# A four-layer graph network on one core: the layers of a pair of batches put off until beside the next pair's extra block

## The chip, the cores and the metric

The kernel runs on one core of a Trainium2 chip. The time is device microseconds of one execution, the median of three runs: 5891.98 us (5891.88 to 5895.87). One further execution was profiled; it took 5867.21 us, and the profile's span of it, from its first to its last recorded instruction, is 5865.4 us.

## The reference

Sixteen batches of a graph with 1024 nodes and 64 features pass four layers, each with a layer norm before it and a residual sum behind it. The first takes quartiles over neighbours, the other three multiply by the adjacency matrix.

```python
h = jnp.maximum(_layernorm(x), 0.0); x = x + L0(h, adj, nodemask, ...)   # quartiles
h = jnp.maximum(_layernorm(x), 0.0); x = x + L1(h, adj, ...)             # gated messages
h = jnp.maximum(_layernorm(x), 0.0); x = x + L2(t, h, adj, ...)          # tanh messages
h = jnp.maximum(_layernorm(x), 0.0); x = x + L3(h, adj, ...)             # attention

def L0(x, adj, mask, ...):
    nd = thinned(adj, mask)                  # every skip-th neighbour is dropped, both ways
    s = sort(where(nd, x, inf))              # per node and feature
    agg = sum(w * lerp(s, tau * (nv - 1)) for tau, w in zip((.25, .5, .75), (.25, .5, .25)))
    return (relu((x + agg) @ W1 + b1) @ W2 + b2) * mask
def L1(h, A, ...):
    m = relu(relu(h @ W1 + b1) @ W2 + b2); msg = relu(A @ m)
    r, z, n = gates(msg @ W_ih.T, h @ W_hh.T); return (1 - z) * n + z * h
def L2(t, h, A, ...):
    return tanh(concat(h, A @ h) @ W1 + b1) @ W2 + b2
def L3(h, adj, W, a):
    hw = h @ W; lh = leaky_relu(hw); e = (lh @ a_src)[:, None] + (lh @ a_dst)[None, :]
    dj = .8 * adj + .2 * e; att = softmax(where(dj > 0, dj, -1e12), axis=1)
    return relu(att @ hw)
```

## The kernel before

The sixteen batches go as eight pairs. Names of the stages in what follows:

- **sort** (`sort_begin`, `sort_pair`, L732 on): for both batches of a pair at once, a sorting network over the nodes on the vector engine, forward with compares (L771 to L775), then backward through the recorded swaps to get each node's code (L803 to L813). It leaves tables of values and codes in DRAM (`h_d`, `p_d`, `t_d`, `w_d`, `y_d`).
- **prepare** (`neighbours`, L858 on), batch after batch: loads the adjacency matrix (`a`, L872), makes 0/1 neighbours and their running count (L873, L878), transposes the matrix on TensorE and stores it in DRAM (`a_d`, L884 to L890), squares the counts on the scalar engine (L907 to L909), and adds up the thinned, symmetric matrix on TensorE (L928, L934) into `ndT`. L945 is the first step behind the last of a batch's matmuls.
- **select** (`weights`, `select`, L960 on), for both batches of the pair: matmuls of `ndT` with position weights (L1096, into PSUM `comb`), evicted on the scalar engine into `y` (L1104), transposed and turned into signs (L1149, L1151); the vector engine takes maxima over `y` (L1162 to L1178, called *lasts* here), and a second family of matmuls (L1196) with masked copies (L1204) picks the values, which are added into `agg` (L1071, L1073). `compact` (L1226 on) gathers the few nodes that fell outside the window and stores their counts in `x_d`.
- **extras** (L1301 on), once a pair: does those few nodes over the full width, for three statistics, and puts the result into `agg` (L1368).
- **layers** (L1374 on), for each batch: the rest of the first layer and the three others. A batch is one chain: L1471 `o0`, L1485 end of layer 0, a pass over the eight blocks of `a_d` (`adj_block`, L1450; matmuls L1459), gates, L1520 end of layer 1, a second pass, L1536 end of layer 2, L1544, then eight attention blocks, each scalar L1561, vector L1563, scalar L1569, vector L1570, scalar L1575, matmuls L1459, and L1583 `x4` with the store of the output.

Program order for pair `pr`: select(pr), extras(pr), layers of both batches, prepare(pr+1), sort of pr+1, `sort_begin` of pr+2. The engines' queues are not written by hand: a scheduler with this order as priority builds one fixed in-order queue for each engine, so that what is traced later fills places where it finds nothing earlier ready. A tile that takes the place of an older one waits for that one tile's users (`reuse_waits="tile"`).

Pools are laid on a stack, so a stage's pools set what may run beside it. In SBUF, bytes per partition: select's `y` stands at 133952 to 170816; extras' pool `xs` at 138016 to 228864; the two batches' layers have a pool each, `ly0` at 138016 to 181696 and `ly1` at 181696 to 228768. In PSUM, select takes all 8 banks; beside prepare (2 banks) extras takes 6, and the layers take 3 and 2 with one for the sort.

## Time and profile before

| | us |
|---|---|
| median of the runs | 5891.98 |
| profiled execution | 5867.21 |
| its span | 5865.4 |
| vector engine (DVE) busy | 5066.1 |
| TensorE (PE) busy | 4372.7 |
| scalar engine (ACT) busy | 3801.4 |
| GpSimd (POOL) busy | 180.9 |
| DMA moved | 568.23 MB, mean 97 GB/s |

A view by windows gives, for any stretch of the span, the busy time of each engine, the TensorE clock that was granted (1 is full), and the share of the DMA engines. A timeline lists an engine's instructions by start, and in brackets how long the engine had been idle before and which instruction ended that. The wait list sums such idle times by the line that waited and the line that released it. Some lines belong to helpers (`norm` L693 to L703, `transposed` L1408 and L1412, `places` L1019 to L1024, `pick` L1064).

The same cycle comes back eight times. The stretch from one pair's first *lasts* instruction to its last is called a **select stretch** here, the one from there to the next pair's first a **tail**: it holds the end of select, extras, layers, prepare and most of the backward sort.

### The profile page before, as it was taken

To read this page: it belongs to the slowest core of one execution; us is meant where nothing else is said; L and a number is where in the kernel's file an instruction comes from. 1 tells how busy PE (TensorE), PEld (TensorE's weight loads), DVE (VectorE), ACT (ScalarE), POOL (GpSimd) and SP (SyncE) were. 2 spreads that over 40 slices of the span, in tenths; PEclk is the share of its full clock that TensorE was granted. 3 is DMA by queue.
4 is the path that set the end of the run, shared out by engine and by line. 5 is a ranking of instruction groups with operands and counts; after the bars stand their busy time and mean duration, and the time that the engine had idled before them with its cause. 6 is when DMAs were issued, how large, how long until landed. Compare 5 with 4: busy or idle time off the path is not lost.

```text
span 5865.4 us, 114417 instructions
## 1 busy us (share of the span) xinstructions
PE 4372.7 (75%) x45010; PEld 2736.6 (47%) x45010; DVE 5066.1 (86%) x13175; ACT 3801.4 (65%) x5752; POOL 180.9 (3%) x292
## 2 busy tenths in 40 slices
PE   1488677885868857788577876788677895878856
PEld 1355443554435544455434554355443554435532
DVE  9899888988899897998889988899888998877744
ACT  1587657676576855777567666677657775577724
POOL 3000000000000000000000000000000000000000
PEclk5699778997889968899689986899878997789967
DMA  4401273013631056210561125501264013620023
GB/s 127 125 27 41 89 221 116 27 31 124 207 98 36 20 156 217 63 40 29 172 203 45 37 77 168 172 35 34 89 206 132 27 32 120 208 81 19 11 88 127
DMA packets 524420, 568.23 MB, mean 97 GB/s; under 512 B 263808, under 2 KB 413568, under 8 KB 523872
## 3 DMA queue, kind: packets, MB, share of 16 engines
q1 hardware_dynamic: 381472, 476.43, 26.0%
q10 hardware_dynamic: 140064, 81.84, 4.6%
q8 instruction: 355, 5.82, 0.4%
q0 software_dynamic: 2336, 2.57, 0.2%
q14 instruction: 193, 1.58, 0.1%
HBM read 376.95 MB, written 183.76 MB: 96 GB/s over the span
## 4 chain that ended last, share of the span: by engine, by line
PE 27%; DVE 23%; ACT 14%; DMA 10%; issue 3%; SPq 0%; POOL 0%; ACTq 0%; DVEq 0%; POOLq 0%
PE comb L1096 7%; DVE y L1167 5%; PE cand L1196 4%; DMA adjT<-a_d 4%; PE bank L1459 4%; ACT sign L1151 3%; PE comb L1287 3%; DMA a_d<-at 2%; ACT y L1104 2%; DVE cand L1204 2%; DVE att L1570 2%; DVE adjT L1563 1%; DVE y L1162 1%; DVE cum L878 1%; DVE wt L974 1%
## 5 line engine op out<-in xcount | busy, mean ns | idle before, releaser
L1096 PE MATMUL comb<-wt,ndT 128*128 128x512 fp8e5 x6144 | 1422.3, 383 | 119.5 <-ACT sign L1151 98.1
L1104 ACT ACTIVATE y<-comb,qb 128x512 int16<-128x512 f32 x1152 | 742.5, 711 | 479.4 <-PE comb L1096 479.0
L1096 PEld LDWEIGHTS <-ndT 128*128 128x128 fp8e5 x6144 | 587.6, 98 | 837.4 <-issue 196.9
L1196 PE MATMUL cand<-vtab,sign 128*128 128x48 f16 (+1 forms) x18432 | 678.8, 192 | 60.9 <-DVE agg L1071 32.4
L1196 PEld LDWEIGHTS <-sign 128*128 128x128 fp8e5 x18432 | 651.5, 97 | 118.6 <-issue 57.2
L1151 ACT ACTIVATE sign<-comb,lower 128x1024 fp8e5<-128x1024 int16 (+1 forms) x640 | 693.2, 1083 | 0.0
L1151 ACT ACTIVATE sign<-comb,half 128x1024 fp8e5<-128x1024 int16 (+1 forms) x640 | 688.0, 1075 | 0.0
L1167 DVE TENSOR_TENSOR y<-y 128x512 uint16<-128x512 uint16 (+5 forms) x896 | 668.7, 788 | 16.6 <-PE comb L1149 16.2
L1204 DVE COPY_PREDICATED cand<-w_f,cand 128x256 f32<-128x256 uint16 (+1 forms) x1536 | 533.7, 376 | 95.8 <-PE cand L1196 92.6
L886 ACT COPY at<-pk 128x512 f32<-128x512 f32 x256 | 147.4, 586 | 394.5 <-PE pk L884 219.0
L1149 PE MATMUL comb<-ident_b,y 128*128 128x128 bf16 x4608 | 318.1, 222 | 93.5 <-ACT sign L1151 59.6
L1459 PE MATMUL bank<-adjT,nd 128*64 128x512 f32 x1024 | 314.1, 668 | 77.6 <-DMA adjT<-a_d 75.7
L1149 PEld LDWEIGHTS <-y 128*128 128x128 bf16 x4608 | 294.6, 99 | 118.9 <-issue 117.9
L928 PE MATMUL pk<-minus_b,rem 128*128 128x128 bf16 x1024 | 225.3, 246 | 158.2 <-ACT rem L909 158.2
L1459 PE MATMUL bank<-att,hs 128*64 128x512 f32 x512 | 199.9, 863 | 155.0 <-ACT hs L1575 154.9
L928 PE MATMUL pk<-ident_b,ni 128*128 128x128 bf16 x1024 | 220.5, 243 | 122.0 <-ACT ndT L934 65.0
L878 DVE TENSOR_TENSOR_SCAN cum<-ni 128x1024 f16<-128x1024 fp8e5 x128 | 291.8, 2283 | 11.0 <-POOL ni L874 10.9
L884 PE MATMUL pk<-ident,a 128*128 128x128 f32 x1024 | 189.5, 336 | 136.8 <-DMA a<-in_adj_dram 102.5
L974 DVE TENSOR_SCALAR wt<-node 128x2048 uint8<-128x2048 f16 x224 | 268.8, 1216 | 13.9 <-PE comb L1287 13.7
L774 DVE TENSOR_TENSOR s<-s 128x512 f32<-128x512 f32 (+1 forms) x440 | 275.6, 626 | 0.0
L1162 DVE TENSOR_SCALAR y<-y 128x4608 int16<-128x4608 int16 x128 | 173.4, 1355 | 118.0 <-ACT y L1104 117.7
L775 DVE TENSOR_TENSOR s<-s 128x512 f32<-128x512 f32 (+1 forms) x440 | 274.4, 624 | 0.0
(373 smaller groups left out, 8301.5 us busy)
## 6 DMA issues: line engine op xcount, KB each, us to landing
adjT<-a_d SPq DMA_DIRECT2D x384, 512.0 KB
a<-in_adj_dram SPq DMA_DIRECT2D x128, 512.0 KB
a_d<-at ACTq DMA_DIRECT2D x256, 256.0 KB
m_d<-swapped SPq DMA_DIRECT2D x104, 512.0 KB
swapped<-m_d SPq DMA_DIRECT2D x104, 512.0 KB
n_d<-nat SPq DMA_DIRECT2D x128, 128.0 KB
x_d<-xr SPq DMA_DIRECT2D x48, 256.0 KB
comb_x<-x_d ACTq DMA_DIRECT2D x24, 512.0 KB
```

The source lines that it names most:

```text
L774: nc.vector.tensor_tensor(to_lo, lo, hi, op=ALU.max)
L878: nc.vector.tensor_tensor_scan(cum[:, t - t0, :], ni[:, t, :], wide[:, t, pad - 1 : pad - 1 + N], 0.0, op0=ALU.add, op1=ALU.add)
L928: nc.tensor.matmul(pk[:, n % 4, :], lhs, rhs, start=(n % 4 == 0 and m == 0), stop=(m == len(terms) - 1 and last),)
L974: nc.vector.tensor_scalar(wt[g][:, :, k : k + 4, :].bitcast(U8), node, 4.0 * (25 + CODE * (8 * g + k)), 4.0 * 26, op0=ALU.add, op1=ALU.min,)
L1096: nc.tensor.matmul(pw, ndT[:, j, t * P : (t + 1) * P], wt[1 + g8][:, j].rearrange("p w c -> p (w c)"), start=(j == 0), stop=(j == NT - 1),)
L1104: nc.scalar.activation(y[:, 0, chunks, at : at + 8 * d_].rearrange("p q (w d) -> p q w d", d=d_), pw.rearrange("p (w q d) -> p q w d", w=8 ...
L1149: nc.tensor.transpose(pt[:, q - q0, :], y[:, 0, q, :].bitcast(BF16), ident_b)
L1151: nc.scalar.activation(signs[tl][s][:, q0:q1, :], pt.bitcast(I16), AF.Sign, bias=before[s], scale=-1.0, saturate=False,)
L1167: nc.vector.tensor_tensor(v[:, :, :, :n], v[:, :, :, :n], v[:, :, :, n : 2 * n], op=ALU.max)
L1196: nc.tensor.matmul(cand[:, e, at : at + 12 * d_].rearrange("p (d l) -> p d l", l=12), signs[tl][sec][:, chunk, :], tab[:, q, :, half_ * 12 ...
L1204: nc.vector.copy_predicated(v[:, :, :, dst : dst + k], mk.to_broadcast([P, 2, C // 2, k]), v[:, :, :, frm : frm + k])
L1459: nc.tensor.matmul(po[to : to + C, :], lhs, rhs[:, f * HALF : (f + 1) * HALF], start=(j == 0), stop=(j == NT - 1))
```

## The change

Extras, layers and the loop over the pairs are rewritten.

- The layers of pair `pr-1` are traced in the tail of pair `pr`, ahead of extras(pr), then prepare and sort as before. In tail 0 there are no layers. In the last tail extras(7) comes first, then the layers of pair 6 with a pool for each batch; behind it the layers of pair 7, again with two pools.
- Where layers run beside extras there is one layer pool, `ly0` (SBUF 132832 to 175808, 2 PSUM banks), which both batches use in turn; extras has `xs` at 175808 to 228320 and 3 banks.
- `agg` goes to DRAM at the end of extras (`g_d`) and is loaded again in layers; `a_d` holds 6 batches, not 4. `rz` takes `att`'s tile; `ones_b` shrinks to 128 columns.
- Extras reads `x_d` in pieces of at most 1024 columns, once for each statistic (12 loads for 4), evicts it in 4 pieces for 1, turns signs in 2 halves for 1, has one `y_x` for two, and works its six sums in groups of four and two: `places` runs twice on narrower words, which lie in the buffers of `comb_x`, and each sum's matmuls and masked copies go in two halves.

What the engines' queues look like afterwards, by the order of the built program: in a middle tail the vector engine has the end of select, then `o0` of the first batch, that batch's chain to `x4` interleaved with extras' first group, prepare and backward sort, then `o0` of the second batch and its chain to `x4` with extras' second group, the rest of prepare, the next pair's weights (L974) and the forward sort of the pair after next, then the first *lasts*. On TensorE the next pair's first L1096 stands behind the transposes (L1581) of the second batch's `x4`; before, L1096 and the second batch's attention matmuls alternated. In a middle pair the scheduler puts 56 us of sort into the select stretch where it put 80 us, and 24 us more into the tail (by the mean durations of before).

```diff
@@ gnn_stack @@
-    a_d = dram.tile([4, NT, P, N], F32, name="a_d")
+    a_d = dram.tile([6, NT, P, N], F32, name="a_d")
+    g_d = [dram.tile([P, NT, C], F32, name=f"g_d{k}") for k in range(4)]
@@ extras @@
-        comb = xs.tile([P, NW * C], F32, name="comb_x")
-        for u in range(0, len(PIECES), 2):
-            nc.scalar.dma_start(comb[:, at], x_d[:, at])
+        def wide():
+            return xs.tile([P, N], F32, name="comb_x", bufs=2)
...
+        def evicted(k):
+            y = xs.tile([P, 2, 2 * NQ, 4 * NH], I16, name="y_x")
+            for u in range(0, len(PIECES), 2):
+                n = len(PIECES[u : u + 2]) * 512
+                comb = wide()[:, :n]
+                nc.scalar.dma_start(comb, x_d[:, PIECES[u] * 512 : PIECES[u] * 512 + n])
+                nc.scalar.activation(y[...], comb.rearrange(...), AF.Identity, bias=qx[:, k : k + 1], scale=1.0)
+            return y
+        def turned(y):
+            signs = [xs.tile([4 * NH, NQ, P], F16, name="sign_x", bufs=4) for s in range(2)]
+            for q0 in range(0, NQ, 8):
+                pt = xp.tile([P, 512], F32, name="tr")...
+                for q in range(8):
+                    nc.tensor.transpose(pt[: 4 * NH, q, :], y[:, 0, q0 + q, :].bitcast(BF16), ident_b)
+                for s in range(2):
+                    nc.scalar.activation(signs[s][:, q0 : q0 + 8, :], pt[: 4 * NH].bitcast(I16), AF.Sign, ...)
+            return signs
...
-        marks = places(xs, z, 6 * C, 1)
-        for s in range(6):
-            cand = xp.tile([P, NQ, P], F32, name="cand")
+        for ks in (range(2), range(2, 3)):
+            for k in ks:
+                y = evicted(k)
+                signs += turned(y)
+                last_of(k - ks[0], y, z, odd)
+            spare = [wide().bitcast(U16) for part in range(-(-10 * nf // (2 * N)))]
+            marks = places(Words(spare, ...), z, nf, 1)
+            for s in range(2 * len(ks)):
+                for q0 in range(0, NQ, 8):
+                    cand = xp.tile([P, 8, P], F32, name="cand")
...
+            if pr + 1 < B // 2:
+                nc.sync.dma_start(g_d[(pr * 2 + i) % 4], aggs[i])
@@ layers @@
+        if agg is None:
+            agg = big()
+            nc.sync.dma_start(agg, g_d[b % 4])
-        rz = ly.tile([P, NT, 2 * C], F32, name="rz")
+        rz = ly.tile([P, N], F32, name="att", bufs=2).rearrange("p (t k) -> p t k", k=2 * C)
@@ the loop over the pairs, behind select @@
-            with nb_ as nb, nbp_ as nbp:
-                with ...(name="xs") as xs, ...(name="xp") as xp:
-                    taken = extras(pr, kept, aggs, xs, xp)
-                with ...("ly0"), ...("ly1"), ...("lb0", bufs=3), ...("lb1", bufs=2), ...("sop", bufs=1):
-                    for i, (ly, lb) in enumerate(((ly0, lb0), (ly1, lb1))):
-                        layers(pr * 2 + i, (pr * 2 + i) % 4, aggs[i], ly, lb)
-                    if pr + 1 < pairs:
-                        made = prepare(pr + 1, nb, nbp)
-                        sort_pair(pr + 1, cur, sop)
-                    if pr + 2 < pairs:
-                        cur = sort_begin(pr + 2, sop)
+        with ExitStack() as beside:
+            final = pr + 1 == pairs
+            if not final:
+                nb, nbp, sop = ...
+            pools = [layer_pools(beside, k, 2) for k in range(2 if final else 1)] if waiting else []
+            xs, xp = ...
+            if final:
+                taken = extras(pr, kept, aggs, xs, xp)
+            if waiting:
+                layers_of(*waiting.pop(), *pools)
+            if not final:
+                taken = extras(pr, kept, aggs, xs, xp)
+                made = prepare(pr + 1, nb, nbp)
+                sort_pair(pr + 1, cur, sop)
+                if pr + 2 < pairs:
+                    cur = sort_begin(pr + 2, sop)
+            waiting.append((pr, aggs if final else [None, None]))
+    with ExitStack() as beside:
+        layers_of(*waiting.pop(), *[layer_pools(beside, k, 4) for k in range(2)])
```

## The prediction

> **What bounds the kernel now.** I read the page's busy line first, then the windows by stage, then the waits inside a tail, then two timelines.
>
> ```profile
> PE 4372.7 (75%) x45010; PEld 2736.6 (47%) x45010; DVE 5066.1 (86%) x13175; ACT 3801.4 (65%) x5752; POOL 180.9 (3%) x292
> ```
>
> No engine is full; the vector engine (DVE) is nearest. The windows below are start:end, length, then busy time of PE, PEld, DVE, ACT, POOL, the granted TensorE clock, DMA share, GB/s. Row 298 is select stretch 0, 641 tail 0, 982 select stretch 1; 2055 and 2392 are a tail and a select stretch of the middle; 5208 is the last select stretch, 5559 the end.
>
> ```profile
> 298.00:641.00 343.00, 298.98 (x3732) 195.34 (x3731) 325.86 (x838) 267.15 (x432) 1.84 (x2) 0.98 0.10 30
> 641.00:982.00 341.00, 234.94 (x1881) 138.89 (x1881) 292.79 (x787) 202.03 (x279) 15.12 (x26) 0.77 0.57 177
> 982.00:1352.00 370.00, 313.16 (x3747) 203.63 (x3745) 335.52 (x858) 272.62 (x442) 1.82 (x3) 0.93 0.09 29
> 2055.00:2392.00 337.00, 229.61 (x1882) 137.00 (x1882) 289.23 (x774) 198.72 (x273) 15.73 (x26) 0.77 0.57 176
> 2392.00:2760.00 368.00, 310.72 (x3744) 201.49 (x3744) 338.76 (x867) 275.69 (x446) 2.02 (x3) 0.94 0.10 32
> 5208.00:5559.00 351.00, 308.49 (x3752) 199.68 (x3751) 264.42 (x715) 276.22 (x447) 1.14 (x2) 0.94 0.06 16
> 5559.00:5865.00 306.00, 184.57 (x1159) 91.75 (x1159) 146.01 (x430) 106.72 (x126) 4.08 (x7) 0.67 0.33 104
> ```
>
> To be seen: DVE idles 48 us in a middle tail (86% busy) and 29 in a select stretch. Select stretch 0, which has no layers beside it, takes 343 with DVE 95% busy; the last takes 351 though DVE has 61 us less to do. So a select stretch is set by its own chain of PE, ACT and DVE, not by the sort work that fills it; what makes the middle ones 368 to 371 is the end of the layers that reaches into them. This is the next view, PE's timeline (start, length; idle before in brackets): the second batch's attention matmuls alternate with the next pair's first matmuls, which evens out two chains that wait for other engines.
>
> ```profile
> 2373.03 0.59 PE L1096 MATMUL comb<-wt,ndT 128*128 128x512 fp8e5 x2
> 2375.04 1.08 PE L1459 MATMUL bank<-att,hs 128*64 128x512 f32 x4 [1.42 <-ACT hs L1575]
> 2376.06 6.65 PE L1096 MATMUL comb<-wt,ndT 128*128 128x512 fp8e5 x30
> 2390.24 0.61 PE L1124 MATMUL comb<-ident_b,ndT 128*128 128x128 bf16 x8
> 2411.11 1.11 PE L1581 MATMUL bank<-ident,srcT 128*128 128x128 f32 x4 [0.70 <-ACT srcT L1578]
> ```
>
> DVE's waits in 2205 to 2392 (waiter, releaser, total us, times, longest) are steps of the layers' chains, though filler stands all around them:
>
> ```profile
> DVE xs L1485 <- PE bank L1478: 5.7, 2, 2.9
> DVE rn L1516 <- ACT rz L1514: 4.9, 4, 1.7
> DVE xs L1536 <- PE bank L1436: 4.2, 1, 4.2
> DVE att L1570 <- ACT att L1569: 2.7, 4, 1.6
> ```
>
> The chain itself, in DVE's timeline of the end, where only the other batch is beside it: `o0`, ends of layers 1 and 2, L1544, `x4`.
>
> ```profile
> 5668.61 0.68 DVE L1471 TENSOR_TENSOR nd<-nd,agg 128x512 f32<-128x512 f32 x1
> 5726.20 0.69 DVE L1520 TENSOR_TENSOR xs<-nd 128x512 f32<-128x512 f32 x1 [0.70 <-ACT nd L1518]
> 5763.47 0.69 DVE L1536 TENSOR_TENSOR xs<-bank,xs 128x512 f32<-128x512 f32 x1 [7.80 <-PE bank L1436]
> 5773.23 0.69 DVE L1544 SCALAR_TENSOR_TENSOR hT<-mT 128x512 f32<-128x512 f32 x1 [4.75 <-ACT mT L1542]
> 5822.22 0.69 DVE L1583 TENSOR_TENSOR nd<-bank,xs 128x512 f32<-128x512 f32 x1 [0.52 <-PE bank L1581]
> ```
>
> That is 154 us; in tails 0 to 6 the first batch took 172, 162, 166, 158, 166, 165, 163 and the second, about 10 us behind, 188 to 196. One batch's chain is thus nearly half a tail, and before, two ran side by side.
>
> **The change, part by part**
>
> *Middle tails (1 to 5).* Both batches now use one pool, so the second `o0` comes after the first `x4`: two chains in series. The start moves forward: `o0` stands in DVE's new order right behind the end of select; the last L1073 of select starts 38 us into the tail (2093.5), so I take 40 (before: 2206.7, 152 in). First chain: the rows give 163 with the other batch beside it; now extras and prepare are beside it. Between its `o0` and `x4` the new order has 155 us of DVE work (every instruction by its mean duration of before), at the 95% of select stretch 0 again 163. Second chain: the shortest of each step over the sixteen batches (9.1, 1.2, 33.7, 7.2, 37.3, 9.7, 49.0) add up to 147; DVE's work there, 120 us, does not bind. Between them 5 us (the order has 7 us of work from `x4` to `o0`). Then the next pair's first L1096, behind L1581 in PE's new order; and the new `y` lies over `ly0`, so its eviction would wait for `x4` in any order. From the first L1096 to L1124, about the first *lasts*, are 17 us above. Sum 40 + 163 + 5 + 147 + 17 = 372. Bounds: 345 (DVE's 331 us of work in this tail at 96%; 24 of its 41 us more are sort that left the select stretch, some 15 layers and weights that did, the rest extras) and 395 (chains of 172 and 160). Five tails: 1860 against 334 + 337 + 332 + 339 + 339 = 1681, +179. Tail 6 has no next sort to begin, the chains are the same: 370 against 332, +38.
>
> *Select stretches 1 to 7.* No layers reach in, and less sort: like stretch 0, 342 each (bounds 335 and 352, the last's). 2394 against 370 + 369 + 368 + 367 + 368 + 371 + 351 = 2564, −170.
>
> *Tail 0.* Layers leave; prepare sets it. Pair 1's first batch reaches L945 at 776, 135 into the tail; the second was 79 behind the first at the start (181 and 260), where no layers ran: 214. Then qb's few steps, first matmuls, 17: some 36. 250 against 341, −91; DVE's work, 226, fits. Bounds 235 and 265.
>
> *The end.* Layers(6) run beside extras(7) in two pools: start 25 in, second batch 190 (its 185 of the last pair, and some for extras): 215. DVE's order puts pair 7's first L1485 behind pair 6's last `x4`, so layers(7) follow whole: from L1485 (5677.9) to the end, 187. 402 against 306, +96. Bounds 380 and 420.
>
> *Extras.* Per pair DVE gets 62 instructions more, at half widths. From L1064 (955 ns at 768 columns, 419 at 256) a column costs 1.05 ns, so the added fixed parts are 60 to 90 ns each: +4 us, inside the 331. ACT: L1325 (3.28 us at 3584) and L1335 (1.96 at 2048) give 0.19 us fixed, so 9 + 6 pieces add 3; 8 more issues at L1307's 0.55 add 4; ACT is busy 199 of 337, so nothing on the path. But the loads now stand in ACT's queue, each waiting for one of two buffers, and the layers' ACT steps are queued behind them; L1325 waited 10.9 us for a landing in six pairs. What hides such waits is ACT's free time, 138 us of a tail; without that cover they cost what the third rival does. SP gets four transfers of 256 KB a pair (`g_d`), written a whole select ahead of their use: nothing; their bound is one landing, 5 us a tail.
>
> *ACT table loads* go from 88 to 100 in the program. By the row of L697 (1283 ns, and 20.4 us idle before 40) that is 12 × 1.8 = 22 us in all, spread over chains: inside the bounds. The Trainium skill, "ScalarE: Activation LUTs", section What ACT_TABLE_LOAD costs, counts a drain too, 2.66 us in all; by it the 12 cost 32 us (an estimate). The idle before the rows is less than that drain.
>
> *A rule that speaks against my sum.* The tail's DVE is busy 86%, the highest of any engine there. The Trainium skill, "Trace Analysis", section Optimization Strategy, says that a kernel with several regimes may gain by interleaving them, and it works from the engine with the highest occupancy; by it the tails would shrink towards DVE's work, 5 × 331 and 302 in tail 6, and the span to 5644 (an estimate). I go by the rows: layers were interleaved already, and DVE still waited on their steps.
>
> **Sum.** +179 + 38 − 170 − 91 + 96 = +52: a span of 5917. The median of the runs is 26.6 above the profiled span (5891.98 − 5865.4), which I add: 5944.
>
> **The rivals**
>
> 1. *DVE packs the tail.* With three independent chains around it filler never lacks, and a tail is DVE's work at the 95.5% of stretch 0: 331 / 0.955 = 347, tail 6 325. Then +54 − 7 − 170 − 91 + 96 = −118: median 5774. For it: extras' stretch 2130 to 2202 is 94% busy. Against: two chains of 147 leave no such tail unless they overlap, and one pool and the order forbid it. It decides where a middle tail is below 361.
> 2. *It cancels:* tails of 362, the same as rival 1 half true: within 12 us of 5892.
> 3. *ACT's queue stalls.* The 12 loads hold ACT until a buffer is free and the third statistic's until DVE's marks in those buffers are used; the first chain stops with it. Loads of this kind took 5 to 8 us in the chain of waits (2098.6: 5.8; 1392.5: 8.0); half of 12 × 6 exposed is 36 a tail, six tails: +216, median 6160; a third of it 6015. For it: ACT's queue is in order. Against: 138 us of free ACT time in a tail.
> 4. *The change does not do what it says* is excluded by the built order.
>
> **How the numbers follow.** About 0.2%, 12 us, is what a measurement of this kernel can tell from no change. Forecast (slower, some 30 to 90 us): 0.53. Rival 1: 0.23. Rival 2: 0.08. Rival 3: 0.16. So faster 0.23, same 0.08, slower 0.69. Six tails at ±14 and seven select stretches at ±5 are ±90 around 5944; with part of the rivals: 5845 to 6050.
>
> **What would show it.** Right: middle tails of 360 to 385 with DVE idle some 40 in them; second `o0` just behind the first `x4`; first L1096 behind the second `x4`; select stretches 335 to 350; an end near 400. Wrong: a lone chain of 130 or less (tail near 345), or idle ACT before L1325's loads in tens of us. If select stretches stay at 368 though no layers reach in, the sort or PE's clock set them, and the sum rises by 180.

## The result and the profile after

The changed kernel takes 6137.93 us (median of four runs, 6118.97 to 6147.62) beside 5891.93 us of the kernel before: a ratio of 1.0419, 95% interval 1.0397 to 1.0442. It is 4.2% slower; the forecast was slower by 0.9%. The profiled execution has a span of 6140.1 us.

Line numbers of the changed kernel are 3 higher in the sort, select and neighbours (L1096 is now L1099, L1162 is L1165); in the layers L1471 is now L1517 (`o0`), L1485 is L1531, L1581 is L1627, L1583 is L1629 (`x4`), and the extras' load and eviction are L1330 and L1331.

The page's busy line after, to be held against the one of before:

```profile
PE 4481.0 (73%) x45010; PEld 2738.8 (45%) x45010; DVE 5114.3 (83%) x13671; ACT 3860.9 (63%) x5884; POOL 201.7 (3%) x292
```

DVE's work grew by 48 us in 275 us of span: the time is in waits. The windows after (start:end, length, busy time of PE, PEld, DVE, ACT, POOL, granted clock, DMA share, GB/s) are, in this order, tail 0, select stretch 1, a middle tail, the select stretch behind it and the end:

```profile
645.00:896.00 251.00, 138.31 (x1486) 103.78 (x1487) 226.49 (x593) 134.59 (x196) 11.01 (x20) 0.65 0.51 151
896.00:1244.00 348.00, 304.01 (x3741) 198.16 (x3737) 326.49 (x841) 267.58 (x433) 2.01 (x3) 0.96 0.10 30
2724.00:3127.00 403.00, 255.25 (x1926) 146.16 (x1926) 332.25 (x905) 217.12 (x309) 18.71 (x26) 0.71 0.54 166
3127.00:3470.00 343.00, 301.59 (x3704) 196.05 (x3701) 302.32 (x798) 265.42 (x428) 2.38 (x3) 0.96 0.08 25
5681.00:6140.00 459.00, 306.55 (x1565) 132.41 (x1565) 230.56 (x756) 190.33 (x247) 6.46 (x13) 0.72 0.43 137
```

Taken from the first and last *lasts* themselves, tail 0 lost 90 us (342 to 251.5) and select stretches 1 to 7 lost 178 together (2555 to 2378). Against that stand six tails of 399 to 403 (before 333 to 340), +386, and the end of 459 (before 306), +153. The sum is +271; select stretch 0 adds 3, and the spans differ by 275. (The forecast's rows of before begin a select stretch about 1 us early, so it has 2564 for 2555 and, for the six tails, 2013 for 2021.) In the middle tail DVE is busy 332 of 403 us, 82%, where it was 86% before.

DVE's timeline of this tail (start, length) shows `o0` and `x4` of the first batch, the same of the second, and the first *lasts* of the next select:

```profile
2773.77 0.69 DVE L1517 TENSOR_TENSOR nd<-nd 128x512 f32<-128x512 f32 x1 [6.52 <-DMA nd<-g_d]
...
2944.79 0.69 DVE L1629 TENSOR_TENSOR nd<-bank,xs 128x512 f32<-128x512 f32 x1 [1.52 <-PE bank L1627]
...
2952.51 0.69 DVE L1517 TENSOR_TENSOR nd<-nd 128x512 f32<-128x512 f32 x1 [0.35 <-DMA nd<-g_d]
...
3114.60 0.69 DVE L1629 TENSOR_TENSOR nd<-bank,xs 128x512 f32<-128x512 f32 x1
...
3127.38 1.35 DVE L1165 TENSOR_SCALAR y<-y 128x4608 int16<-128x4608 int16 x1
```

The tail is one row of steps: 50 us, a chain of 171, 8 us, a chain of 162, 13 us. The second `o0` comes 8 us behind the first `x4`. PE's timeline at the end of the second chain has the next pair's first comb matmul starting half a microsecond behind the start of its last transposes:

```profile
3113.20 0.66 PE L1627 MATMUL bank<-ident,srcT 128*128 128x128 f32 x4 [0.70 <-ACT srcT L1624]
3113.70 4.48 PE L1099 MATMUL comb<-wt,ndT 128*128 128x512 fp8e5 x20
```

### The profile page after: what moved, and what is told of

It is laid out like the page before. It is cut to its first block, busy times and chain, and to the rows that moved or that the text cites. A ratio compares the mean times of both kernels' runs of the same rounds, so it can differ in the third digit from the quotient of the medians.

```text
span 6140.1 us, 115258 instructions
## 1 busy us (share of the span) xinstructions
PE 4481.0 (73%) x45010; PEld 2738.8 (45%) x45010; DVE 5114.3 (83%) x13671; ACT 3860.9 (63%) x5884; POOL 201.7 (3%) x292
## 3 DMA queue, kind: packets, MB, share of 16 engines
q0 software_dynamic: 2336, 2.57, 0.2%
## 4 chain that ended last, share of the span: by engine, by line
PE 36%; DVE 30%; ACT 17%; DMA 13%; issue 3%; POOL 0%; SPq 0%; ACTq 0%; DVEq 0%; POOLq 0%
PE comb L1099 12%; DMA adjT<-a_d 6%; PE cand L1199 6%; ACT sign L1154 5%; DVE y L1170 5%; PE bank L1502 4%; PE comb L1290 4%; DVE cum L881 3%; ACT y L1107 2%; DMA a_d<-at 2%; DVE att L1616 2%; DVE cand L1207 2%; DVE adjT L1609 1%; DVE s L777 1%; DVE s L778 1%
## 5 line engine op out<-in xcount | busy, mean ns | idle before, releaser
L1099 PE MATMUL comb<-wt,ndT 128*128 128x512 fp8e5 x6144 | 1427.5, 385 | 111.7 <-ACT sign L1154 95.7
L1099 PEld LDWEIGHTS <-ndT 128*128 128x128 fp8e5 x6144 | 591.7, 98 | 824.1 <-issue 195.9
L1199 PE MATMUL cand<-vtab,sign 128*128 128x48 f16 (+1 forms) x18432 | 666.4, 191 | 43.2 <-DVE agg L1076 29.2
L1199 PEld LDWEIGHTS <-sign 128*128 128x128 fp8e5 x18432 | 637.4, 96 | 102.0 <-issue 37.1
L1502 PE MATMUL bank<-att,hs 128*64 128x512 f32 x512 | 232.0, 1009 | 355.9 <-ACT hs L1621 355.8
L1502 PE MATMUL bank<-adjT,nd 128*64 128x512 f32 x1024 | 363.8, 796 | 127.2 <-DMA adjT<-a_d 122.8
L1165 DVE TENSOR_SCALAR y<-y 128x4608 int16<-128x4608 int16 x128 | 173.4, 1355 | 184.9 <-ACT y L1107 184.4
L977 DVE TENSOR_SCALAR wt<-node 128x2048 uint8<-128x2048 f16 x224 | 264.7, 1218 | 14.9 <-PE comb L1290 14.6
L778 DVE TENSOR_TENSOR s<-s 128x512 f32<-128x512 f32 (+1 forms) x440 | 274.3, 623 | 0.0
```

The source lines that it names most:

```text
L778: nc.vector.tensor_tensor(to_hi, lo, hi, op=ALU.min)
L1099: nc.tensor.matmul(pw, ndT[:, j, t * P : (t + 1) * P], wt[1 + g8][:, j].rearrange("p w c -> p (w c)"), start=(j == 0), stop=(j == NT - 1),)
L1199: nc.tensor.matmul(cand[:, e, at : at + 12 * d_].rearrange("p (d l) -> p d l", l=12), signs[tl][sec][:, chunk, :], tab[:, q, :, half_ * 12 ...
L1502: nc.tensor.matmul(po[to : to + C, :], lhs, rhs[:, f * HALF : (f + 1) * HALF], start=(j == 0), stop=(j == NT - 1))
```

## The experiments

Each kernel ran beside the kernel before on the same chip. Ratios are to that kernel; where none is given there was one run. "Tail", "select stretch" and "end" are as in the forecast, and "period" is a middle tail with the select stretch behind it: 705 us in the kernel before, 741 in the changed one. Means of five are over tails 1 to 5 and the select stretches behind them.

### What sets a tail

**no_second** leaves out the layers of the odd batch of pairs 0 to 5.

```diff
-        for i in range(2):
+        for i in range(2 if len(pools) > 1 else 1):
             layers(pr * 2 + i, (pr * 2 + i) % 6, aggs[i], *pools[i % len(pools)])
```

> The changed kernel without the layers of the second batch of pairs 0 to 5 (their rows of the output are not computed): the six late tails hold one chain in place of two. Theory (two chains in series set the tail): each of the six tails loses a whole second chain until another limit is met, 401 down to about 305, total about 5570 us. Rival (the vector engine's work sets the tail): each loses only the vector engine's work of one batch's layers, some 40 us, total about 5900 us.

5594.18 us. Its middle tail, in the windows:

```profile
2543.00:2851.00 308.00, 197.61 (x1692) 123.55 (x1693) 265.67 (x727) 174.48 (x251) 13.96 (x23) 0.72 0.56 168
```

A tail falls by 92 us, 401 to 309 (means), though DVE's work in a period falls by only 42 (634 to 592): the second chain is on the path. The theory's 305 is met, the rival's 5900 is not.

**noext_one** and **noext_two** leave out the extras and their pools; only the store to `g_d` stays. The first keeps the one pool, the second has two side by side.

```diff
     def extras(pr, kept, aggs, xs, xp):
+        for i in range(2):
+            if pr + 1 < B // 2:
+                nc.sync.dma_start(g_d[(pr * 2 + i) % 4], aggs[i])
+        return None
```

and, in noext_two alone,

```diff
-            pools = [layer_pools(beside, k, 2) for k in range(2 if final else 1)] if waiting else []
+            pools = [layer_pools(beside, k, 2) for k in range(2 if final else 2)] if waiting else []
```

> The changed kernel without the extras (flagged nodes keep the value of the select; only the store of agg to g_d is left), so that two chains in series have only prepare, sort and select's rest beside them. Theory (two chains in series set the tail): tails of 370 to 395 us although 30 to 45 us of the vector engine's work are gone, total 5950 to 6080 us. Rival (the vector engine's work and the extras beside the first chain set it): tails fall by the extras' work or more, below 350 us, total below 5800 us.

> The changed kernel without the extras, in whose place stands a second pool for the layers in the middle tails: two chains side by side, put off by one pair. Theory: tails of 290 to 330 us, 60 us or more below those of the same kernel with one pool, total 5500 to 5650 us; so what the one pool costs is the difference. Rival (the late start and other limits set the tail, not the series of chains): within 20 us a tail of the same kernel with one pool.

5970.0 and 5558.1 us. The same tail and select stretch in the windows of noext_one:

```profile
2656.00:3056.00 400.00, 240.11 (x1430) 125.36 (x1431) 343.77 (x840) 190.05 (x280) 16.05 (x26) 0.70 0.50 159
3056.00:3385.00 329.00, 296.40 (x3733) 194.47 (x3731) 259.83 (x706) 267.93 (x433) 1.46 (x3) 0.98 0.06 16
```

and of noext_two:

```profile
2514.00:2828.00 314.00, 220.27 (x1430) 119.02 (x1431) 263.93 (x702) 186.08 (x278) 17.12 (x26) 0.78 0.60 185
2828.00:3171.00 343.00, 299.44 (x3739) 195.75 (x3734) 326.17 (x838) 267.72 (x433) 1.81 (x2) 0.98 0.10 31
```

With one pool a tail is 400 us with or without extras (401 and 398 on average), although the extras' work is gone. The scheduler fills the time with sort that otherwise stands in the select stretch (DVE 344 and 260), which is 15 us shorter than with two pools. With two pools the tail is 315. So one pool costs 83 us a tail, 412 us in all. The extras beside the row cost 4 us of a middle tail and 14 of a period (741 to 727); of the 168 us in all between 6138 and 5970, 44 are in tail 0 and 51 in the end. The tails of noext_one are on average 3 us above the upper end of what was expected; its total and both numbers of noext_two are as expected.

**bank_shared** is the kernel before with one PSUM pool of five banks for both layer chains, in place of three and two; SBUF pools stay apart.

```diff
-                    tc.tile_pool(reuse_waits="tile", name="lb0", bufs=3, space=PSUM) as lb0,
-                    tc.tile_pool(reuse_waits="tile", name="lb1", bufs=2, space=PSUM) as lb1,
+                    tc.tile_pool(reuse_waits="tile", name="lb0", bufs=5, space=PSUM) as lb0,
...
-                    for i, (ly, lb) in enumerate(((ly0, lb0), (ly1, lb1))):
+                    for i, (ly, lb) in enumerate(((ly0, lb0), (ly1, lb0))):
```

> The kernel before with one pool of five banks for both layer chains in place of three and two. If banks bound the chains: the second falls to 175 to 183 us, total 5830 to 5880 us. If a bank that the other chain still holds costs as much as it gives (banks are taken in turn): 5884 us within 12, or slower.

6610.61 us, ratio 1.1255 (1.1233 to 1.1278). DVE's timeline (both `o0`, first `x4`, the second batch's first step behind a bank, second `x4`; L1471, L1485 and L1583 are as in the kernel before):

```profile
2393.88 0.68 DVE L1471 TENSOR_TENSOR nd<-nd,agg 128x512 f32<-128x512 f32 x1
...
2403.57 0.68 DVE L1471 TENSOR_TENSOR nd<-nd,agg 128x512 f32<-128x512 f32 x1
...
2547.68 0.69 DVE L1583 TENSOR_TENSOR nd<-bank,xs 128x512 f32<-128x512 f32 x1 [1.20 <-PE bank L1581]
...
2555.73 0.69 DVE L1485 TENSOR_TENSOR xs<-bank,mask 128x512 f32<-128x512 f32 x1 [4.23 <-PE bank L1478]
...
2691.32 0.69 DVE L1583 TENSOR_TENSOR nd<-bank,xs 128x512 f32<-128x512 f32 x1 [4.32 <-PE bank L1581]
```

The second batch has its `o0` 10 us behind the first, as before. Its first matmul (PE L1408) then starts at 2547.43, 0.9 us behind the start of the first batch's last transposes (PE L1581, 2546.52), and its next step on DVE comes 152 us behind its `o0`. Tails grow from 337 to 467 (means of five), select stretches fall from 367 to 330, as no layers reach into them. The expectation has the sign only, as its last words, "or slower". What the run shows is the changed kernel's loss made by itself, without any put-off: a pool that two chains use in turn puts them in series. Here shared PSUM banks alone did it; in the changed kernel SBUF and PSUM are both shared, and which of the two holds the second chain there was not separated.

### Why 401 and not 372

**x_on_sp** issues the twelve loads of `x_d` on SP's queue.

```diff
-                nc.scalar.dma_start(comb, x_d[:, PIECES[u] * 512 : PIECES[u] * 512 + n])
+                nc.sync.dma_start(comb, x_d[:, PIECES[u] * 512 : PIECES[u] * 512 + n])
```

> The changed kernel with the twelve loads of x_d per pair issued on SP's queue in place of ACT's. Theory (length of two chains in series): nothing waits for ACT's queue, so 6138 us within 20. Rival (ACT's queue stalls behind these loads): 100 us or more faster, all of it in the first chain of a tail, 172 falling to 155 or less.

6087.91 us, ratio 1.0342 (1.0305 to 1.0379), below the changed kernel's interval: both expectations missed, and the result lies between them. ACT's timeline in the changed kernel shows what was held up:

```profile
2765.62 1.32 ACTq L1330 DMA_DIRECT2D comb_x<-x_d  x2
...
2774.58 2.19 ACT L1331 ACTIVATE y_x<-comb_x,qx 128x1024 int16<-128x1024 f32 x2 [9.39 <-DMA adjT<-a_d]
```

ACT issued two loads and then stood 9.4 us until L1331 could evict them (the releaser's name is inferred; the loads are the ones issued 9 us before). Middle tails are now 389 to 396 (400 to 403 before the edit). In them, on average, the second chain is 154 where it was 161, the first 171 where it was 172, the start 45 where it was 48, with `o0` waiting at most 1.0 us for `agg` out of `g_d` in place of 4.4 to 6.5. The rival put the gain into the first chain; it came in the second.

**noext_one5** is noext_one with five banks of PSUM for the one pool, not two.

```diff
-            pools = [layer_pools(beside, k, 2) for k in range(2 if final else 1)] if waiting else []
+            pools = [layer_pools(beside, k, 2 if final else 5) for k in range(2 if final else 1)] if waiting else []
```

> The changed kernel without the extras, one layer pool in the middle tails as in the run with one pool (5970 us, chains 176 and 152, tails near 398), but five banks of PSUM for it in place of two. If two banks are what makes the chains 10 to 13 us longer than the rows of before showed (163 and 147, with three banks): chains of 165 and 145, tails near 380, total 5850 to 5900 us. If the work beside them does it: 5970 us within 25.

5909.95 us: middle tails of 382 to 389, chains of 166 to 169 and 148 to 153, in place of 175 to 180 and 150 to 159. On average the third to fifth banks are worth 9 us of the first chain and 4 of the second. That is nearer to the first expectation, 5 us a tail and 10 in all above its numbers. With five banks in the one pool a tail is still 385 us, 70 above the 315 of two pools with two banks each: most of what the one pool costs is the series of the chains, not the number of banks.

**three** takes both from the changed kernel: loads on SP's queue, and a third bank for the layers, got by drawing candidates for four tables at a time.

```diff
-                for q0 in range(0, NQ, 8):
-                    cand = xp.tile([P, 8, P], F32, name="cand")
-                    for q in range(8):
+                for q0 in range(0, NQ, 4):
+                    cand = xp.tile([P, 4, P], F32, name="cand")
+                    for q in range(4):
...
-                    here = slice(q0 * 4, (q0 + 8) * 4)
+                    here = slice(q0 * 4, (q0 + 4) * 4)
...
-            pools = [layer_pools(beside, k, 2) for k in range(2 if final else 1)] if waiting else []
+            pools = [layer_pools(beside, k, 2 if final else 3) for k in range(2 if final else 1)] if waiting else []
```

> The changed kernel with the loads of x_d on SP's queue (as in the run at 6088 us) and a third bank of PSUM for the one layer pool, which comes from candidates drawn in pieces of four tables in place of eight. If loads and banks are the 29 us by which a middle tail missed the sum: chains of 160 to 165 and 147 to 150, middle tails of 370 to 382, total 6010 to 6050 us. If the banks matter only where no extras are beside the chains: 6088 us within 15.

6071.46 us, ratio 1.0317 (1.0296 to 1.0339). DVE's timeline of the same tail (start 2711.0, first *lasts* 3093.6):

```profile
2754.52 0.69 DVE L1517 TENSOR_TENSOR nd<-nd 128x512 f32<-128x512 f32 x1 [1.78 <-DMA nd<-g_d]
...
2917.86 0.69 DVE L1629 TENSOR_TENSOR nd<-bank,xs 128x512 f32<-128x512 f32 x1 [0.89 <-PE bank L1627]
...
2926.46 0.69 DVE L1517 TENSOR_TENSOR nd<-nd 128x512 f32<-128x512 f32 x1 [1.62 <-DMA nd<-g_d]
...
3080.83 0.69 DVE L1629 TENSOR_TENSOR nd<-bank,xs 128x512 f32<-128x512 f32 x1 [1.07 <-PE bank L1627]
```

43.5 + 163.3 + 8.6 + 154.4 + 12.8 = 382.6. The first chain is the forecast's 163; the middle tails (384 on average) are just above what was expected; the total misses it by 21 us; tail 0 (263) and the end (469) are 11 and 9 us longer than in the changed kernel. As total times, three and x_on_sp are not told apart (their intervals overlap); the bank shows in the lengths of one execution each: on average the first chain is 164 us where it was 171, and a middle tail 384 where it was 392. (The candidates' pieces changed with the bank; noext_one5, where there are none, changed the banks alone.) The Trainium skill, "Perfetto Trace Analysis", section Matmuls, says that independent groups should rotate through different PSUM banks so that one is evacuated while the next is computed; the bank's 7 us in the first chain agree.

**bank_swap** gives the kernel before two banks for the first batch and three for the second.

```diff
-                    tc.tile_pool(reuse_waits="tile", name="lb0", bufs=3, space=PSUM) as lb0,
-                    tc.tile_pool(reuse_waits="tile", name="lb1", bufs=2, space=PSUM) as lb1,
+                    tc.tile_pool(reuse_waits="tile", name="lb0", bufs=2, space=PSUM) as lb0,
+                    tc.tile_pool(reuse_waits="tile", name="lb1", bufs=3, space=PSUM) as lb1,
```

> The kernel before with the five banks of PSUM of its two layer pools given the other way: two to the first batch's, three to the second's. If a third bank shortens a chain by 7 to 15 us wherever the chain stands: first chain 172 to 178 in place of 163, second 175 to 183 in place of 190, so the select stretches, into which the second chain reaches, 360 in place of 368: total 5830 to 5870 us. If the second chain is long because it always stands behind the first on the engines: lengths unchanged or the first simply slower, 5884 us within 12 or more than that.

5908.97 us, ratio 1.0059 (1.0041 to 1.0077). In tails 1 to 6 the first chain went from 158 to 167 up to 168 to 176 (means 164 and 172), the low end of what was expected, at the same granted clock (0.81 in one chain of each); the second stayed (188 to 197 beside 188 to 196). The total is that of the second expectation. A third bank shortened the chain that leads, not the one that stands 10 us behind it. So the 163 that the forecast took for its first chain was a row of three banks.

### What the put-off and the pieces are worth

**ext_alone** is the kernel before with the new `extras` and nothing else: its diff is the part of the change's diff under extras, without the store to `g_d`. **ext_sp** is ext_alone with the edit of x_on_sp.

> The kernel before with nothing but the new form of the extras (pieces of half the size, two statistics and then one, loads through two buffers); layers stay in their own pair's tail, in two pools. It prices the new form where the layers wait for it. Theory (long chains, extras cheap): 60 added vector instructions and a longer row of steps cost up to 20 us a tail, total 5900 to 6030 us. Rival A (the new form itself is the loss): the extras' stretch, 72 us before, grows by 60 us or more in each of eight tails, total 6300 us or more; it would also explain why, with half of the layers put off, the on-time batch began some 65 us later than in the kernel before. Rival B (costs nothing): 5888 us within 12.

> The kernel before with the new form of the extras alone (6230 us), with its loads of x_d on SP's queue. In that kernel the on-time layers began 213 us into a tail, 61 later than before. If the loads in ACT's queue are that delay: 150 us less or more, below 6080 us. If it is the form itself (one statistic after the other through two buffers and one y_x): 6230 us within 60.

6229.75 us, ratio 1.0605 (1.0586 to 1.0625), and 6328.52 us. The window of ext_alone between the end of select and the first `o0`:

```profile
2195.00:2369.00 174.00, 80.63 (x918) 67.06 (x919) 158.24 (x423) 105.31 (x144) 9.80 (x17) 0.60 0.55 171
```

The layers wait for the extras here, and their `o0` comes 212 us into a tail on average, where it came 154 in before: 58 us for the pieces (12 loads through two buffers, one `y_x`, `places` twice). A tail is 391 us in place of 337, a period 753 in place of 705. The total lies outside the theory's range and below rival A's 6300, but the mechanism is rival A's. On SP's queue the start is no earlier (212 too), so ACT's queue is not the delay there, and other steps grow: L1485 to L1502 by the lines of before, where the first transposed adjacency is needed, takes 44 us in place of 33 in the first batch, and the second chain 201 in place of 191. The Trainium skill, "DMA: Bandwidth & Descriptors", section Issuing engines are not separate DMA queues, says that starting transfers from several engines at once saves only the time it takes to initiate them. In these runs the same twelve loads moved from ACT to SP took some 45 us off the changed kernel (4.19% less 3.42% of before) and put some 100 on ext_alone (one run). The step L1485 to L1502 went along: in ext_alone it grew by 11 us, in the changed kernel's second chain it fell from 42 to 37.

So the change is two losses and a gain: pieces that cost 351 us where layers wait for them, a put-off that takes most of that off the path, and one pool that puts the chains in series.

### Where the pool lies

**swap** enters the extras' pools ahead of `ly0` in the middle tails, so that `ly0` no longer lies under the next select's `y`.

```diff
-            pools = [layer_pools(beside, k, 2) for k in range(2 if final else 1)] if waiting else []
+            if final:
+                pools = [layer_pools(beside, k, 2) for k in range(2)]
             xs, xp = ...
+            if not final:
+                pools = [layer_pools(beside, 0, 2)] if waiting else []
```

> The changed kernel with the order of two allocations exchanged in the middle tails, so that the layers' pool lies above the extras' pool and no longer under the next select's y tiles, and its two banks of PSUM are the last two. If the second chain holds the next select's start by the memory it lies in, part of its end may now overlap the select: tails and selects together 0 to 60 us shorter in all, 6080 to 6140 us. If PE's order alone holds the start (first comb matmul behind the last transposes of x4), no change: 6138 us within 15.

6091.01 us (two runs), ratio 1.0343 (1.029 to 1.0396). A tail and select stretch of it:

```profile
2722.00:3082.00 360.00, 241.81 (x1868) 141.23 (x1869) 288.90 (x819) 200.19 (x284) 18.92 (x26) 0.74 0.57 175
3082.00:3461.00 379.00, 317.14 (x3760) 202.28 (x3759) 345.46 (x882) 282.15 (x453) 1.74 (x3) 0.92 0.11 33
```

From pair 2 on the tails are 41 us shorter and the select stretches 39 longer: 739 a period beside 741. The next select now starts beside the second chain's end (32 us ahead of its `x4`) and takes longer there. Where the boundary falls gave 2 us a period; the two chains' row did not get shorter. Of the 34 us by which the profiled execution is faster, 14 are in the last tail and its select stretch and 8 in the end. The total is in the range of the first expectation.

### Other ways of putting off

**half** puts off only the second batch `b` of a pair, beside the next pair's extras, and runs that pair's first batch in a second pool behind them, then prepare and sort; **half_sp** has the loads on SP's queue as well.

```diff
+            if waiting:
+                late = layer_pools(beside, 0, 2)
+            with ...xs, ...xp:
+                taken = extras(pr, kept, aggs, xs, xp)
+                if waiting:
+                    layers(b, b % 6, None, *late)
+            first_ = layer_pools(beside, 1, 3)
+            layers(pr * 2, (pr * 2) % 6, aggs[0], *first_)
...
```

> The changed kernel with only the second batch of each pair put off: a tail runs the extras of its pair first, beside them the layers of the second batch of the pair before (pool ly0), and then the layers of the pair's own first batch in a second pool where the extras' pool was. Theory (a middle tail of 401 us is two layer chains end to end, 172 + 161, plus start and end): here the two chains overlap, because they use two pools, and a tail falls to 345 to 355 us; select stretches 342 to 368; the end about 315; total 5830 to 5900 us. Rival (the extras' new loads in ACT's queue hold the chains up): tails of 385 or more whatever the number of pools, total above 6000 us.

> The kernel with half of the layers put off (6167 us), with the twelve loads of x_d on SP's queue. If the loads in ACT's queue hold up layers and extras alike: 50 us less, as in the changed kernel (6138 to 6088), so about 6115 us. If the loads lie on the path of the extras, which here gate the on-time batch: 100 us less or more, 6070 us or below. If neither: 6167 us within 15.

6166.8 us, ratio 1.048 (1.0445 to 1.0515), and 6093.0 us, ratio 1.0366 (1.0333 to 1.0399). DVE's timeline of a tail of half that starts at 2097.4 (late `o0`, on-time `o0`, late `x4`, on-time `x4`):

```profile
2144.76 0.69 DVE L1517 TENSOR_TENSOR nd<-nd 128x512 f32<-128x512 f32 x1 [4.77 <-DMA nd<-g_d]
...
2313.55 0.69 DVE L1517 TENSOR_TENSOR nd<-nd,agg 128x512 f32<-128x512 f32 x1
...
2346.09 0.69 DVE L1629 TENSOR_TENSOR nd<-bank,xs 128x512 f32<-128x512 f32 x1 [0.74 <-PE bank L1627]
...
2488.07 0.69 DVE L1629 TENSOR_TENSOR nd<-bank,xs 128x512 f32<-128x512 f32 x1 [1.07 <-PE bank L1627]
```

The expectation was wrong. It forgot that the on-time batch needs this pair's extras, which in pieces end 216 us into the tail, much as in ext_alone: the chains overlap for 33 us only, and the second reaches 26 us into the select. The rival's tail of 385 is not there either (353 to 365 in tails 1 to 6). Beside the kernel before, the span is 297 us longer: 148 in tails 1 to 6, 86 in the end (393, where 315 was expected), 40 in tail 0 and 23 in the select stretches. Loads on SP's queue took 1.1% off, between the two numbers expected.

**late_two** puts the late pair side by side in two pools and the old `extras` behind it in the same memory; **late_end** has also another end (the last extras beside the two put-off layers in one pool, then the last pair's own layers in two more pools); **late_hp** is late_end with the extras in `tc.high_priority()`.

```diff
+            with ...sop:
+                layers_of(*waiting.pop(), *[layer_pools(inner, k, 3 - k) for k in range(2)])
+                made = prepare(pr + 1, nb, nbp)
+                sort_pair(pr + 1, cur, sop)
+                cur = sort_begin(pr + 2, sop)
+            with ...xs, ...xp:
+                taken = extras(pr, kept, aggs, xs, xp)
```

> A kernel that keeps the put-off but not the shared memory: in each tail the layers of the pair before run first, both batches side by side in two pools (three and two banks), beside prepare and sort; after them, in the same memory, the extras of the pair in the form of the kernel before. Theory (two chains in series are the loss, a late pair side by side takes 209 us from 48 us into the tail, the old extras 72 us, then 17 to the next select): middle tails of 335 to 360 us, selects 342, first tail 250 to 260, end 440 to 480: total 5750 to 5900 us. Rival (the extras behind the layers hold up the next select and cost as much as the series of chains): tails of 390 us or more, total above 6050 us.

> The kernel with the late pair side by side and the old extras behind it, with another end: the last pair's extras stand beside the two put-off layers in one pool, and the last pair's own layers follow the extras in two more pools, so that four chains overlap. Theory: an end of 370 to 410 us in place of about 460, so 50 to 90 us less than the kernel with the late pair side by side. If the four chains share an engine that is full: no gain, within 15 us.

> The kernel with the late pair side by side, old extras behind it and the other end (6230 us), with the extras ahead of the sort's work in the order of the vector engine. If what cost it 427 us a tail was sort work standing ahead of the extras (the vector engine was full from 2350 us on): tails of 345 to 365, sort's work moves into the selects, 345 to 370, total 5850 to 5980 us. If the series of chains and extras sets the tail by itself: tails of 400 or more still, total above 6100 us.

6306.53 us, ratio 1.0734 (1.071 to 1.0759); 6230.42, 1.0603 (1.0578 to 1.0628); 6276.22, 1.0657 (1.0634 to 1.0681). Middle tails of 422 to 433: late_two's theory was wrong and its rival right, and late_hp came out as its second expectation said in number. The late pair ended about 270 us into the tail (257 expected); the other 160 are in the windows of late_hp behind it and in DVE's groups from 2336 to 2496:

```profile
2370.00:2420.00 50.00, 11.17 (x124) 9.63 (x124) 47.17 (x117) 19.67 (x14) 0.00 (x0) 0.56 0.18 38
2420.00:2470.00 50.00, 13.86 (x320) 12.98 (x320) 49.76 (x97) 0.00 (x0) 0.00 (x0) 0.50 0.11 44
```

```profile
L977 DVE TENSOR_SCALAR wt<-node 128x2048 uint8<-128x2048 f16 x18 | 21.7, 1220 | 0.0
L776 DVE TENSOR_TENSOR swapped<-s 128x512 uint16<-128x512 f32 (+1 forms) x31 | 20.7, 666 | 0.5
L777 DVE TENSOR_TENSOR s<-s 128x512 f32<-128x512 f32 (+1 forms) x30 | 20.0, 666 | 0.0
L778 DVE TENSOR_TENSOR s<-s 128x512 f32<-128x512 f32 (+1 forms) x30 | 20.0, 666 | 0.0
```

DVE is full there, with 61 us of the forward sort (L776 to L778) and 22 of the next weights (L977) around the extras' steps, while PE is busy 25 us of 100. Tails now hold 362 us of DVE's work and select stretches 276, and the select stretches, at 337, hardly got shorter for it. A priority for the extras did not shorten the tails (430 where they were 424). That the sort's work in this place is the loss is argued from these rows, not shown: whether a schedule that leaves it to the select stretch would gain was not tried. The other end did what was expected: 407 us in place of 487. None of the kernels that do all of the work beats the kernel before.

## Why the forecast was right in sign and wrong in size

- *Select stretches 342 each:* right. Stretches 1 to 7 sum to 2378 (forecast 2394); with the layers gone from them each is 25 us shorter.
- *Tail 0, 250:* 251.5, but for another reason than given. Without extras it is 207 (noext_one), so the extras, and not prepare alone, set it. (The forecast's reading of L945, 776, is 772.7 in the trace.)
- *Two chains in series, the second `o0` behind the first `x4`, the first comb matmul behind the second:* right, and shown three ways: without the second chain the tail is 309, with two pools (and no extras) 315, and the same series made in the kernel before costs 130 us a tail, of which the select stretch gives 37 back.
- *The sum of a middle tail, 40 + 163 + 5 + 147 + 17 = 372:* this is the step that failed. It measured 48.0 + 171.6 + 7.8 + 161.2 + 12.8, in all 401.5 (means of tails 1 to 5, the parts rounded), outside even its upper bound of 395. The terms that were mis-sized are the chains' lengths, 163 by 9 and 147 by 14, and the start by 8. They were read from rows that did not hold for the new place. The 163 came from a pool with three banks (two now); with a third bank, in three, the first chain is 164. The 147 was the shortest of every step over chains that had no loads in ACT's queue behind them. Step by step, with the lines of before, the second chains had 42 us from L1485 to L1502 (forecast 35), 10 for the gates (7) and 53 for the attention blocks (49); with the loads on SP's queue the first of these is 37 and the chain 154. With both edits the tail is 384. Of the 12 us still missing 7 are the second chain's, 154, which is 149 without extras and with five banks; how these 7 divide was not separated (in the last 53 us of that chain, 3062 to 3115, DVE is busy 52). A sum of shortest steps is a bound, not a length.
- *The total, 5917 for the span and 5944 with the 26.6 us by which the runs stood above it:* the span came out 223 us longer, 177 of them in the six tails, 57 in the end, 5 in tail 0 and select stretch 0, less 16 in the select stretches. The 26.6 us were not there: the median of the runs is 2 us below the profiled span.
- *`g_d` costs nothing, at most one landing of 5 us a tail:* the first `o0` of tails 1 to 6 waited 4.3 to 6.5 us for a landing, 5 on average (the row above names `g_d`), so the bound came true and is most of the 8 us by which the start was late. In x_on_sp the wait is at most 1.0 us, though only the loads of `x_d` moved; why was not tried.
- *The end, 402:* 459. The term is 25 + 190 for pair 6, which measured 265 up to pair 7's first L1531 (5945.7 − 5680.9); pair 7's own 187 measured 194. Extras(7) beside layers(6) are what was underpriced: without extras the end is 408 to 417.
- *Extras cost +4 us of DVE and nothing on the path:* DVE's work grew by 48 us in eight pairs, 6 a pair. (The forecast's two numbers of L1064 give a fixed part of about 150 ns, 419 − 256 × 1.05, and not 60 to 90.) On the path it was right in the middle tails (401 with all of the extras, 398 without), though a select stretch is 11 us longer with them; it was wrong in the end. And it holds only because the put-off hides them: where the layers wait for the pieces, they begin 58 us later and a period is 48 us longer.
- *Rival 1, DVE packs the tail:* fell. DVE is 82% busy, and without the extras, 31 us of its work in a period, the tail stayed at 398. (Its 325 for tail 6 does not follow from its own terms, 302 / 0.955 = 316.) The rule on interleaving regimes, 5644 us by its estimate, fell with it. The Trainium skill, "Perfetto Trace Analysis", has in the same section (Optimization Strategy) a sentence that fits better: repeated bubbles can mean that there is not enough SBUF or PSUM for the next tile. Here one pool in place of two cost 83 us a tail.
- *Rival 3, ACT's queue stalls:* its mechanism is there at a fifth of the loss: loads on SP's queue take some 45 of 246 us off.

Left open: what holds a tail at 309 to 315 us when the chains are not in series (DVE is 84 to 86% busy there). The last step before the next select is prepare's there: in noext_two the second batch's L948 (L945 before) comes 288 us into the tail, behind 9.6 us in which DVE waited for its matmuls, in no_second 283 us in, behind 5.9. What makes prepare that late was not tried.

## What to carry to other kernels

When work is moved to where it shares half the memory, first ask which chains that used to run side by side will now take turns in one pool, of SBUF or of PSUM, and price them end to end; work beside them hides behind the row, and taking it away gives little back: here 14 us of a period of 741. Read a chain's length from a place with as many banks and the same queue as the new one, and take means, not the best of each step. A block made smaller to fit elsewhere should be timed in its old place first: here the pieces alone cost 351 us, more than the whole change.

## What the runs showed of the hardware that was not expected

- The granted clock fell to 0.50 in the 50 us in which PE had 14 us of work (late_hp, 2420 to 2470), and rose to 0.96 to 0.98 in select stretches, where PE is busy 87 to 90%. In the changed kernel the middle tail's clock is 0.71 where it was 0.77, and a matmul of the layers with the transposed adjacency took 796 ns on average where it took 668: the longer rows of waits and the slower matmuls come together; which makes which was not tried. A lower clock alone did not go with a longer first chain: 163 us at 0.74 in three (2754 to 2918) beside 166 at 0.81 in the kernel before (2207 to 2373).
- The same twelve loads a pair, moved from ACT's to SP's queue, gave some −45 us in the changed kernel and some +100 in the kernel with the pieces alone: no rule for one queue or the other follows from that.
- Two banks in place of three cost a leading chain 7 to 9 us of 164 (x_on_sp beside three, bank_swap beside the kernel before), and a chain that follows another by 10 us nothing that could be seen (bank_swap).
